# Eight units in flight with tiles laid over one another, and new dates for the last units, in a four-layer graph kernel

One core of one Trainium2 chip. The metric is the device time of one launch in microseconds (us), as the median of several runs. All runs quoted here are of the fast state.

## The reference, cut

Sixty-four graphs of 256 nodes with 128 features go through four layers. Each adds its result to its input and normalises over the features. All is float32.

```
x: (64, 256, 128), adj: (256, 256) zeros and ones
layer 0: h = x Wo; attention scores from a pairing of h.a1 and h.a2, masked, softmax over rows; att h + x Ws
layer 1: h = x W; softmax(leaky_relu(h.a_src + h.a_dst) masked by adj or itself) h; elu
layer 2: five steps of a gated unit:  m = adj h;  z, r = sigmoid(...m..., ...h...);
         hv = tanh(...m..., U5 (r h));  h = (1 - z) h + z hv
layer 3: x W0 + sum over k of adj^k x Wk, k = 1..3
after each layer: x = layernorm(x + layer(x))
```

## The kernel before

A **unit** is two graphs. A **lane** is a set of tiles that holds one unit through all four layers; seven lanes mean seven units in flight. The program is straight-line code. Before it is emitted, a greedy planner in Python puts all instructions in order. For each engine it keeps planned times. When an engine is free, it takes the ready task with the smallest date, `first(t)`. When the last task of a unit is done, its lane gets the next unit. PSUM is the memory that TensorE writes its results to; its eight banks are handed out by the planner in the same way.

```
LANES = 7
LAST_FAR = {0: -1, 1: -1}   # last unit, last but one: the state is turned by TensorE, not by DMA
PERIOD = 43e3
TAIL = 0.1
...
def first(t):                                   # the date of a task: smallest first
    ...
    return (t.unit - (1 - TAIL) * max(t.unit - (NU - LANES), 0)) * PERIOD + t.due
...
zs = [cell(f"z{k}", [P, T]) for k in range(LANES)]          # a tile of its own for each lane's input
...
def spawn(u, lane):
    for k, layer in enumerate((layer0, layer1, layer2, layer3)):
        layer(u, lanes[lane])
        if k == (1 if u < LANES else 0) and u + LANES < NU:
            load_x(u + LANES, after=...)        # next input of this lane: asked for early
...
def lane_cells(k):                              # cut: each name a tile of its own
    c = {name: cell(f"{name}_{k}", [P, T]) for name in ("xT0", "xT1", "ht", "m")}
    c |= {name: cell(f"{name}_{k}", [P, G, N]) for name in ("e", "p")}
    for name, (at, half) in {"r": ("e", 0), "z": ("e", 1), "v": ("p", 0)}.items():
        c[name] = Cell(...)                     # halves of e and p
    c["x"] = cell(...); c["h0"] = cell(f"h0_{k}", [P, G, C0])
```

`t.due` is a task's planned distance from the start of its unit, stretched by up to 1.9. A unit's date is thus its number times 43 us, and the last units' dates are pressed together.

The softmax here doesn't subtract the row's maximum and nothing guards it: scores larger than these inputs give would overflow.

Of the kernel before, what the change touches and what calls it, by code (L numbers as in the profile page):

```python
# [8 lines left out]
F32 = mybir.dt.float32  # L9
AF = mybir.ActivationFunctionType  # L10
ALU = mybir.AluOpType
# [3 lines left out]
NEG = -1.0e30  # L15
EPS = 1e-5
STEPS = 5
LANES = 7
LEAD = 10
BANKS = 8  # L20
BL = 32
FIRST_FAR = {0: 2, 1: 2}
LAST_FAR = {0: -1, 1: -1}
PERIOD = 43e3
TAIL = 0.1
PACE = 1.9
PACE_GATED = 1.56
HOLD = 80
# [6 lines left out]
class Cell:  # L35


    def __init__(self, ap=None, bank=False):
        self.ap, self.bank = ap, bank
        self.writers, self.readers, self.users = [], [], 0  # L40
        self.group, self.waits = None, set()

# [10 lines left out]
class Plan:  # L53
# [17 lines left out]
    def add(self, eng, ns, fn, reads=(), writes=(), after=(), wait=0, group=None, dma=False):  # L71
        t = Task(eng, ns, fn, self.unit, wait, dma or eng == "sp")
        for c in reads:
            t.deps.update(c.writers)
            c.readers.append(t)
        for c in writes:
            if c.bank and not c.writers:
                t.takes.append(c)
            if group is None or c.group is not group:
                c.waits = {*c.writers, *c.readers} - {t}  # L80
                c.writers, c.readers, c.group = [], [], group
            t.deps.update(c.waits)
            c.writers.append(t)
        t.deps.update(after)
        t.deps.discard(t)
        for c in {id(c): c for c in (*reads, *writes) if c.bank}.values():
            c.users += 1
            t.banks.append(c)
        t.step = self.step = self.step + 1
        t.layer = self.layer  # L90
        t.rank = self.rank
        self.tasks.append(t)
        return t
# [4 lines left out]
    def run(self, spawn, units, key):  # L98
# [20 lines left out]
            seen = len(self.tasks)  # L119

        def start(lane):
            if queue:
                self.unit, self.step = queue.pop(0), 0
                lane_of[self.unit] = lane
                spawn(self.unit, lane)

                for t in self.tasks[seen:]:
                    t.due = max([d.due + (PACE_GATED if t.layer == 2 else PACE) * (d.ns + (
                        d.wait + self.LATENCY["sp" if d.dma else d.eng] if d.dma or d.eng != t.eng else self.OWN[t.eng]))
                        for d in t.deps if d.unit == t.unit], default=0.0)  # L130
                enlist()
# [50 lines left out]
def kernel(  # L182
# [55 lines left out]
        return n * (cols * 1.667 + 5)  # L238


    def load(name, src, shape, ns=450, by="sp"):
        c = cell(name, shape)
        queue = {"sp": nc.sync, ACT: nc.scalar}[by]
        add(by, ns, lambda: queue.dma_start(c.ap, src), (), (c,), dma=True)
        return c
# [3 lines left out]
    out_u = out.rearrange("(u b) (c p) d -> u p b c d", b=UB, p=P)  # L249


    zs = [cell(f"z{k}", [P, T]) for k in range(LANES)]

    def load_x(u, by="sp", after=()):
        z = zs[u % LANES]
        if u < LANES:
            queue = {"sp": nc.sync, ACT: nc.scalar}[by]
            add(by, 600, lambda: queue.dma_start(z.ap.rearrange("p (b c d) -> p b c d", b=UB, c=NC), x_u[u]), (), (z,), dma=True, wait=800)
            return
        parts = object()  # L260
        for a in range(D // BL):
            add("sp", 540, lambda a=a: nc.sync.dma_start(
                z.ap[a * BL : (a + 1) * BL].rearrange("j (b i) -> j b i", i=BL),
                x_a[u, a].rearrange("(b j) i -> j b i", j=BL)), (), (z,), after, group=parts)

    w1 = load("w1", W, [D, D])
    load_x(0, ACT)
# [162 lines left out]
    plan.rank = None  # L430


    def lane_cells(k):
        c = {name: cell(f"{name}_{k}", [P, T]) for name in ("xT0", "xT1", "ht", "m")}

        c |= {name: cell(f"{name}_{k}", [P, G, N]) for name in ("e", "p")}
        for name, (at, half) in {"r": ("e", 0), "z": ("e", 1), "v": ("p", 0)}.items():
            c[name] = Cell(c[at].ap.rearrange("p g n -> p (g n)")[:, half * T : (half + 1) * T])
        c["x"] = cell(f"x_{k}", [P, UB, NC, D])
        c["h0"] = cell(f"h0_{k}", [P, G, C0])  # L440
        c |= {name: cell(f"{name}_{k}", [P, G]) for name in ("nm", "s", "rs", "rstd", "ve")}
        c |= {name: cell(f"{name}_{k}", [P, UB]) for name in ("d", "nd")}
        c["st"] = cell(f"st_{k}", [P, UB, 6])
        c["u"] = cell(f"u_{k}", [P, 15])
        c["cu"] = cell(f"cu_{k}", [P, 3, G])
        c["esd"] = cell(f"esd_{k}", [P, 2, G])
        c["hb"] = Cell(dram.tile([P, T], F32, tag=f"hb_{k}", name=f"hb_{k}"))

        for name, n in (("row", T), ("rowu", 2 * T + 2)):
            c[name] = Cell(dram.tile([1, n], F32, tag=f"{name}_{k}", name=f"{name}_{k}"))  # L450
        return c


    X = {}
    lanes = [lane_cells(k) for k in range(LANES)]

    def gd(ap):
        return ap.rearrange("p (g d) -> p g d", g=G)
# [88 lines left out]


    def layer0(u, L):
        xT, z = L["xT0"], zs[u % LANES]  # L550
        if u < LANES:
            feature_major(z, lambda g: gd(z.ap)[:, g], xT)
        else:
# [93 lines left out]
    def layer1(u, L):  # L647
# [17 lines left out]
                    ps_x.ap[:, b * N : (b + 1) * N], X[u].ap[:, b, jc, :], p.ap[:, b * NC + jc, :],  # L665
                    start=(b == 0 and jc == 0), stop=(jc == NC - 1), skip_group_check=True), (X[u], p), (ps_x,))
        add(ACT, 500, lambda: nc.scalar.copy(px.ap, ps_x.ap), (ps_x,), (px,))
        rs, hp, hn, th = L["rs"], L["ht"], L["m"], L["xT1"]
        ex = L["h0"]
        exf = ex.ap.rearrange("p g d -> p (g d)")[:, 0:T]  # L670
        for b in range(UB):
            ps_o = bank()

# [3 lines left out]
            for ic in range(NC):  # L677
# [1 line left out]
                    ov()[:, ic, :], bn(px.ap)[:, b, ic * P : (ic + 1) * P], wx1.ap,  # L679
                    start=(ic == 0), stop=True, skip_group_check=True), (px, wx1), (ps_o,))  # L680
            r = rs.ap[:, b * NC : (b + 1) * NC].rearrange("p (c o) -> p c o", o=1)
            add(DVE, 120, lambda r=r, ov=ov: nc.vector.reciprocal(r, ov()[:, :, D : D + 1]), (ps_o,), (rs,), group=exf)
            add(DVE, 350, lambda b=b, r=r, ov=ov: nc.vector.tensor_mul(
                gd(hp.ap)[:, b * NC : (b + 1) * NC, :], ov()[:, :, 0:D], r.to_broadcast([P, NC, D])), (ps_o, rs), (hp,), group=exf)
        if not u:
            plan.rank = NU
            warm(6, [plan.tasks[-1]])
# [1 line left out]

        add(DVE, 330, lambda: nc.vector.tensor_scalar_min(hn.ap, hp.ap, 0.0), (hp,), (hn,))  # L690
        add(ACT, 550, lambda: nc.scalar.activation(th.ap, hn.ap, AF.Tanh, scale=0.5), (hn,), (th,))
        add(ACT, 550, lambda: nc.scalar.activation(exf, hn.ap, AF.Exp), (hn,), (ex,))
        xf = X[u].ap.rearrange("p b c d -> p (b c d)")
        add(DVE, 600, lambda: nc.vector.scalar_tensor_tensor(hp.ap, hp.ap, 0.0, xf, op0=ALU.max, op1=ALU.add),
            (hp, X[u]), (hp,))
        add(DVE, 600, lambda: nc.vector.scalar_tensor_tensor(th.ap, exf, 1.0, th.ap, op0=ALU.add, op1=ALU.mult),
            (ex, th), (th,))
        add(DVE, 600, lambda: nc.vector.tensor_add(hp.ap, hp.ap, th.ap), (hp, th), (hp,))
        layernorm(u, L, y_pairs(hp))
# [130 lines left out]
    def spawn(u, lane):  # L830
        for k, layer in enumerate((layer0, layer1, layer2, layer3)):
            plan.layer = k
            layer(u, lanes[lane])

            if k == (1 if u < LANES else 0) and u + LANES < NU:
                load_x(u + LANES, after=[plan.tasks[-1]] if k else ())



    def first(t):  # L840
        if t.rank is not None:
            return t.rank * PERIOD
        if t.unit < 0:
            return t.due - 1e6
        return (t.unit - (1 - TAIL) * max(t.unit - (NU - LANES), 0)) * PERIOD + t.due

    with tc.manual_schedule():
        for t in plan.run(spawn, range(NU), first):
# [31 lines left out]
```

## Time and profile before

| | before |
|---|---|
| time | 1434.65 us (1432.92 to 1435.07, 3 runs) |
| span of the profiled run | 1433.4 us |
| TensorE busy | 1419.3 us, 99% |
| VectorE, ScalarE, DMA | 78%, 50%, some 45% |
| records of matmuls and transposes | 5665 |

The engine shares, the windows and the chain around the largest wait are shown in the prediction. To follow where the time goes I use one more reading of the trace: for each matmul, the time from its start to the next matmul's start, less the usual one for its shape (429 ns for 512 columns, 216 for 256, 109 to 113 for 128 to 133; the lower quartile of each shape). What is left over I call **excess**: it holds waits as well as matmuls slowed by a lower clock. The usual times sum to 1409.7 us before.

One line is needed later. It is the view of one source line: the VectorE transpose with which layer 0 of a unit begins (all units but the first seven). The last two numbers before the shape are the first and last start.

```profile
L554 DVE STREAM_TRANSPOSE xT<-z x25: 671/702/706, 183.2 to 1266.2; 128x512 f32<-128x512 f32 x25
```

The last unit begins at 1266.2 us, 167.2 us before the end.

### The profile page before, as it was taken

To read this page: it belongs to the slowest core of one execution; us is meant where nothing else is said; L and a number is where in the kernel's file an instruction comes from. 1 tells how busy PE (TensorE), PEld (TensorE's weight loads), DVE (VectorE), ACT (ScalarE), POOL (GpSimd) and SP (SyncE) were. 2 spreads that over 40 slices of the span, in tenths; PEclk is the share of its full clock that TensorE was granted. 3 is DMA by queue.
4 is the path that set the end of the run, shared out by engine and by line. 5 is a ranking of instruction groups with operands and counts; after the bars stand their busy time and mean duration, and the time that the engine had idled before them with its cause. 6 is when DMAs were issued, how large, how long until landed. Compare 5 with 4: busy or idle time off the path is not lost.

```text
span 1433.4 us, 18429 instructions
## 1 busy us (share of the span) xinstructions
PE 1419.3 (99%) x5665; PEld 960.5 (67%) x5665; DVE 1118.8 (78%) x2597; ACT 718.4 (50%) x1372; POOL 142.1 (10%) x134
## 2 busy tenths in 40 slices
PE   9999999999999999999999999999999999999998
PEld 9666766766666666666666666666666666666676
DVE  7987968788778888778888778887788787677735
ACT  5656445445554545554545545445545454455431
POOL 0110100110001110011110011100011010010102
PEclk9999999999999999999999999999999999999999
DMA  3225564544555454554445454444444444423212
GB/s 93 46 46 109 110 141 102 116 97 107 108 113 123 92 120 102 112 117 111 109 100 115 107 122 111 101 103 104 107 108 105 98 103 93 97 70 81 52 37 59
DMA packets 515170, 141.57 MB, mean 99 GB/s; under 512 B 445056, under 2 KB 481664, under 8 KB 515072
## 3 DMA queue, kind: packets, MB, share of 16 engines
q1 hardware_dynamic: 514272, 139.87, 43.8%
q8 instruction: 46, 0.75, 0.2%
q14 instruction: 52, 0.43, 0.1%
q10 hardware_dynamic: 800, 0.52, 0.1%
HBM read 78.21 MB, written 62.10 MB: 98 GB/s over the span
## 4 chain that ended last, share of the span: by engine, by line
PE 97%; DVE 1%; ACT 1%; issue 0%; POOL 0%; POOLq 0%; DVEq 0%; ACTq 0%
PE ps L726 48%; PE ps L706 23%; PE ps L812 8%; PE ps L634 4%; PE ps L664 4%; PE ps L819 4%; PE ps L678 2%; PE ps L567 2%; PE ps L629 2%; PE ps L781 0%; PE ps L472 0%; ACT e L653 0%; DVE st L526 0%; PE ps L299 0%; PE ps L515 0%
## 5 line engine op out<-in xcount | busy, mean ns | idle before, releaser
L726 PE MATMUL ps<-m,gT 128*128 128x512 f32 x960 | 464.6, 595 | 1.4 <-ACT m L722 1.4
L531 POOL TENSOR_TENSOR rstd<-ve,nhalf 128x4 f32<-128x4 f32 x128 | 141.4, 1108 | 1286.6 <-DVE ve L528 1198.3
L726 PEld LDWEIGHTS ps<-m,gT 128*128 128x128 f32 x960 | 176.3, 190 | 137.1 <-issue 110.5
L706 PE MATMUL ps<-adjTp,ht 128*128 128x256 f32 x928 | 231.0, 380 | 0.0
L706 PEld LDWEIGHTS ps<-adjTp,ht 128*128 128x128 f32 x928 | 176.3, 191 | 65.2 <-issue 42.8
L722 ACT COPY m<-ps 128x512 f32<-128x512 f32 x160 | 93.0, 583 | 182.0 <-PE ps L706 179.0
L741 ACT ACTIVATE e<-ps,bias 128x512 f32<-128x512 f32 x160 | 109.9, 687 | 147.1 <-PE ps L726 147.0
L732 ACT ACTIVATE e<-ps,bias 128x512 f32<-128x512 f32 x160 | 109.7, 687 | 142.2 <-PE ps L726 142.2
L745 DVE TENSOR_TENSOR p<-p,xT 128x512 f32<-128x512 f32 x160 | 109.4, 686 | 85.6 <-ACT p L739 85.4
L734 DVE SCALAR_TENSOR_TENSOR e<-e,xT 128x512 f32<-128x512 f32 x160 | 109.1, 683 | 80.0 <-ACT e L732 72.1
L726 PE MATMUL ps<-xT,gT 128*128 128x512 f32 x320 | 162.8, 593 | 2.7 <-DVE esd L639 2.7
L726 PE MATMUL ps<-e,u5T 128*128 128x512 f32 x320 | 162.8, 592 | 0.0
L739 ACT ACTIVATE p<-ps,bias 128x512 f32<-128x512 f32 x160 | 110.0, 687 | 66.4 <-PE ps L726 59.3
L706 PE MATMUL ps<-adjT,x 128*128 128x256 f32 x512 | 128.8, 379 | 0.0
L706 PEld LDWEIGHTS ps<-adjT,x 128*128 128x128 f32 x512 | 96.2, 190 | 44.9 <-issue 34.2
L746 DVE SCALAR_TENSOR_TENSOR p<-e,p 128x512 f32<-128x512 f32 x160 | 109.2, 683 | 2.0
L748 DVE SCALAR_TENSOR_TENSOR xT<-p,xT 128x512 f32<-128x512 f32 x160 | 109.2, 684 | 1.9
L726 PEld LDWEIGHTS ps<-e,u5T 128*128 128x128 f32 x320 | 60.1, 190 | 38.5 <-issue 28.0
L756 DVE STREAM_TRANSPOSE p<-xT 128x512 f32<-128x512 f32 x116 | 81.2, 701 | 1.2
L726 PEld LDWEIGHTS ps<-xT,gT 128*128 128x128 f32 x320 | 57.1, 190 | 36.6 <-issue 23.7
L653 ACT ACTIVATE e<-m,esd 128x256 f32<-128x256 f32 x112 | 80.4, 763 | 0.4 <-DMA m<-row 0.4
L526 DVE BATCH_NORM_STATS2 st<-ps 128x6 f32<-128x256 f32 x128 | 51.5, 424 | 37.0 <-PE ps L819 22.2
(139 smaller groups left out, 1852.2 us busy)
## 6 DMA issues: line engine op xcount, KB each, us to landing
hb<-p SPq DMA_DIRECT2D x174, 256.0 KB, 2.3
ht<-hb SPq DMA_DIRECT2D x464, 64.0 KB, 2.5
xT<-hb SPq DMA_DIRECT2D x232, 64.0 KB, 2.6
m<-row SPq DMA_DIRECT2D x56, 256.0 KB, 3.9
hb<-p SPq DMA_DIRECT2D x120, 64.0 KB, 1.8
ht<-hb SPq DMA_DIRECT2D x30, 256.0 KB, 2.8
out_dram<-x SPq DMA_DIRECT2D x29, 256.0 KB, 2.7
z<-in_x_dram SPq DMA_DIRECT2D x100, 64.0 KB, 2.4
```

What stands on the lines that cost most here:

```text
L531: add(POOL, 1050, lambda: nc.gpsimd.tensor_tensor(rstd.ap, ve.ap, nhalf.ap, op=ALU.pow), (ve, nhalf), (rstd,))
L706: add(PE, mm_ns(N), lambda b=b, mc=mc: nc.tensor.matmul(ps.ap[:, b * N : (b + 1) * N], lhs(b, mc), mat.ap[:, mc, :], start=(mc == 0), stop ...
L722: add(ACT, 500, lambda ps_m=ps_m: nc.scalar.copy(m.ap, ps_m.ap), (ps_m,), (m,))
L726: add(PE, mm_ns(T), lambda: nc.tensor.matmul(ps.ap, w(), rhs.ap, start=start, stop=stop, skip_group_check=True), (c, rhs), (ps,))
L732: add(ACT, 600, lambda ps_g=ps_g: nc.scalar.activation(r.ap, ps_g.ap, AF.Tanh, bias=bias2.ap[:, 1:2], scale=0.5), (ps_g, bias2), (r,))
L734: add(DVE, 600, lambda h=h: nc.vector.scalar_tensor_tensor(r.ap, r.ap, 1.0, h.ap, op0=ALU.add, op1=ALU.mult), (r, h), (r,))
L739: add(ACT, 600, lambda ps_v=ps_v: nc.scalar.activation(v.ap, ps_v.ap, AF.Tanh, bias=bias2.ap[:, 2:3]), (ps_v, bias2), (v,))
L741: add(ACT, 600, lambda ps_g=ps_g: nc.scalar.activation(z.ap, ps_g.ap, AF.Tanh, bias=bias2.ap[:, 0:1], scale=0.5), (ps_g, bias2), (z,))
L745: add(DVE, 600, lambda h=h: nc.vector.tensor_sub(v.ap, v.ap, h.ap), (v, h), (v,))
L746: add(DVE, 600, lambda: nc.vector.scalar_tensor_tensor(v.ap, z.ap, 1.0, v.ap, op0=ALU.add, op1=ALU.mult), (v, z), (v,))
L748: add(DVE, 600, lambda h=h, new=new: nc.vector.scalar_tensor_tensor(new.ap, v.ap, 0.5, h.ap, op0=ALU.mult, op1=ALU.add), (v, h), (new,))
L812: add(PE, mm_ns(N), lambda k=k, src=src, c=c, b=b: nc.tensor.matmul(view(c)[:, :, b, :], bn(src.ap)[:, b, c * P : (c + 1) * P], w3.ap[:, k ...
```

## The change

Its intent: more units in flight, so that TensorE always finds something ready. Eight lanes with a tile for each name do not fit: the build of the old kernel with eight lanes stops with

```
Not enough space for pool "const" with 214.0625 kb per partition ... There was 207.8740234375 kb per partition left
```

This agrees with the Trainium skill, "SBUF — State Buffer", Specifications (TRN2), which gives about 208 KiB as usable. So tiles with disjoint lifetimes are laid over one another. `Cell` learns of overlaps (`over`), and a writer waits for the users of all cells that overlap.

```diff
-LANES = 7
+LANES = 8
-LAST_FAR = {0: -1, 1: -1}
+LAST_FAR = {0: -1, 1: 1}
-TAIL = 0.1
+TAIL = 0.3
+LATE = 5
@@ Cell, Plan.add
-                c.waits = {*c.writers, *c.readers} - {t}
+                c.waits = {w for o in (c, *c.over) for w in (*o.writers, *o.readers)} - {t}
@@ Plan.run, start: a lane now takes only the units u with u % LANES == lane
-            if queue:
-                self.unit, self.step = queue.pop(0), 0
+            mine = [u for u in queue if u % LANES == lane]
+            if mine:
+                self.unit, self.step = mine[0], 0
+                queue.remove(self.unit)
@@ lanes: h0 shares with ht; r, ex and z, th are halves of e; v and xT1 are halves of p
-        c = {name: cell(f"{name}_{k}", [P, T]) for name in ("xT0", "xT1", "ht", "m")}
+        c = {name: cell(f"{name}_{k}", [P, T]) for name in ("xT0", "m")}
+        wide = sb(f"ht_{k}", [P, G * C0])
+        c["ht"] = Cell(wide[:, 0:T])
+        c["h0"] = Cell(wide.rearrange("p (g d) -> p g d", g=G), over=[c["ht"]])
+        for at, halves in (("e", (("r", "ex"), ("z", "th"))), ("p", (("v",), ("xT1",)))): ...
@@ the input lies in m and is asked for at the unit's end
-    zs = [cell(f"z{k}", [P, T]) for k in range(LANES)]
-        z = zs[u % LANES]
+        z = lanes[u % LANES]["m"]
-            if k == (1 if u < LANES else 0) and u + LANES < NU:
-                load_x(u + LANES, after=[plan.tasks[-1]] if k else ())
+        if u + LANES < NU:
+            load_x(u + LANES)
@@ dates
-        return (t.unit - (1 - TAIL) * max(t.unit - (NU - LANES), 0)) * PERIOD + t.due
+        return (t.unit if t.unit < NU - LANES else NU - 1 - LATE - (NU - 1 - t.unit) * TAIL) * PERIOD + t.due
```

The dates of units 24 to 31, in periods, are 24.0, 25.0, 25.1 ... 25.6 by the old formula with seven lanes, 24.0, 24.1 ... 24.7 by the old formula with eight, and 23.9, 24.2, 24.5 ... 26.0 by the new one.

The tie of units to lanes is needed because the input now lies in a tile of the lane. It is one more difference between the two kernels, but no rival. The planner runs without the chip: run again for the kernels of the old rule that are quoted here, it gives unit `u` to lane `u % LANES` anyway, and in the kernels of the new rule the lane that is waited for is also the first to be free.

More of the change, by code (lines that the diff above doesn't have):

```diff
@@ L35, with __init__ @@
 class Cell:
-    def __init__(self, ap=None, bank=False):
+    def __init__(self, ap=None, bank=False, over=()):
         self.ap, self.bank = ap, bank
+        self.over = list(over)
+        for c in over:
+            c.over.append(self)
         self.writers, self.readers, self.users = [], [], 0
@@ L238, in mm_ns, with lane_cells @@
         return n * (cols * 1.667 + 5)
+    def lane_cells(k):
+        c = {name: cell(f"{name}_{k}", [P, T]) for name in ("xT0", "m")}
+        wide = sb(f"ht_{k}", [P, G * C0])
+        c["ht"] = Cell(wide[:, 0:T])
+        c["h0"] = Cell(wide.rearrange("p (g d) -> p g d", g=G), over=[c["ht"]])
+        c |= {name: cell(f"{name}_{k}", [P, G, N]) for name in ("e", "p")}
+        for at, halves in (("e", (("r", "ex"), ("z", "th"))), ("p", (("v",), ("xT1",)))):
+            for half, names in enumerate(halves):
+                over = [c[at]]
+                for name in names:
+                    c[name] = Cell(c[at].ap.rearrange("p g n -> p (g n)")[:, half * T : (half + 1) * T], over=over)
+                    over = [*over, c[name]]
+        c["x"] = cell(f"x_{k}", [P, UB, NC, D])
+        c |= {name: cell(f"{name}_{k}", [P, G]) for name in ("nm", "s", "rs", "rstd", "ve")}
+        c |= {name: cell(f"{name}_{k}", [P, UB]) for name in ("d", "nd")}
+        c["st"] = cell(f"st_{k}", [P, UB, 6])
+        c["u"] = cell(f"u_{k}", [P, 15])
+        c["cu"] = cell(f"cu_{k}", [P, 3, G])
+        c["esd"] = cell(f"esd_{k}", [P, 2, G])
+        c["hb"] = Cell(dram.tile([P, T], F32, tag=f"hb_{k}", name=f"hb_{k}"))
+        for name, n in (("row", T), ("rowu", 2 * T + 2)):
+            c[name] = Cell(dram.tile([1, n], F32, tag=f"{name}_{k}", name=f"{name}_{k}"))
+        return c
+    lanes = [lane_cells(k) for k in range(LANES)]
     def load(name, src, shape, ns=450, by="sp"):
@@ L249, with load_x @@
     out_u = out.rearrange("(u b) (c p) d -> u p b c d", b=UB, p=P)
-    zs = [cell(f"z{k}", [P, T]) for k in range(LANES)]
-    def load_x(u, by="sp", after=()):
-        z = zs[u % LANES]
+    def load_x(u, by="sp"):
+        z = lanes[u % LANES]["m"]
         if u < LANES:
@@ L263, in load_x @@
                 z.ap[a * BL : (a + 1) * BL].rearrange("j (b i) -> j b i", i=BL),
-                x_a[u, a].rearrange("(b j) i -> j b i", j=BL)), (), (z,), after, group=parts)
+                x_a[u, a].rearrange("(b j) i -> j b i", j=BL)), (), (z,), group=parts)
     w1 = load("w1", W, [D, D])
@@ L430 @@
     plan.rank = None
-    def lane_cells(k):
-        c = {name: cell(f"{name}_{k}", [P, T]) for name in ("xT0", "xT1", "ht", "m")}
-        c |= {name: cell(f"{name}_{k}", [P, G, N]) for name in ("e", "p")}
-        for name, (at, half) in {"r": ("e", 0), "z": ("e", 1), "v": ("p", 0)}.items():
-            c[name] = Cell(c[at].ap.rearrange("p g n -> p (g n)")[:, half * T : (half + 1) * T])
-        c["x"] = cell(f"x_{k}", [P, UB, NC, D])
-        c["h0"] = cell(f"h0_{k}", [P, G, C0])
-        c |= {name: cell(f"{name}_{k}", [P, G]) for name in ("nm", "s", "rs", "rstd", "ve")}
-        c |= {name: cell(f"{name}_{k}", [P, UB]) for name in ("d", "nd")}
-        c["st"] = cell(f"st_{k}", [P, UB, 6])
-        c["u"] = cell(f"u_{k}", [P, 15])
-        c["cu"] = cell(f"cu_{k}", [P, 3, G])
-        c["esd"] = cell(f"esd_{k}", [P, 2, G])
-        c["hb"] = Cell(dram.tile([P, T], F32, tag=f"hb_{k}", name=f"hb_{k}"))
-        for name, n in (("row", T), ("rowu", 2 * T + 2)):
-            c[name] = Cell(dram.tile([1, n], F32, tag=f"{name}_{k}", name=f"{name}_{k}"))
-        return c
     X = {}
-    lanes = [lane_cells(k) for k in range(LANES)]
     def gd(ap):
@@ L549, in layer0 @@
     def layer0(u, L):
-        xT, z = L["xT0"], zs[u % LANES]
+        xT, z = L["xT0"], L["m"]
         if u < LANES:
@@ L667, in layer1 @@
         add(ACT, 500, lambda: nc.scalar.copy(px.ap, ps_x.ap), (ps_x,), (px,))
-        rs, hp, hn, th = L["rs"], L["ht"], L["m"], L["xT1"]
-        ex = L["h0"]
-        exf = ex.ap.rearrange("p g d -> p (g d)")[:, 0:T]
+        rs, hp, hn, th = L["rs"], L["ht"], L["m"], L["th"]
+        ex, parts = L["ex"], object()
         for b in range(UB):
@@ L681, in layer1 @@
             r = rs.ap[:, b * NC : (b + 1) * NC].rearrange("p (c o) -> p c o", o=1)
-            add(DVE, 120, lambda r=r, ov=ov: nc.vector.reciprocal(r, ov()[:, :, D : D + 1]), (ps_o,), (rs,), group=exf)
+            add(DVE, 120, lambda r=r, ov=ov: nc.vector.reciprocal(r, ov()[:, :, D : D + 1]), (ps_o,), (rs,), group=parts)
             add(DVE, 350, lambda b=b, r=r, ov=ov: nc.vector.tensor_mul(
-                gd(hp.ap)[:, b * NC : (b + 1) * NC, :], ov()[:, :, 0:D], r.to_broadcast([P, NC, D])), (ps_o, rs), (hp,), group=exf)
+                gd(hp.ap)[:, b * NC : (b + 1) * NC, :], ov()[:, :, 0:D], r.to_broadcast([P, NC, D])), (ps_o, rs), (hp,), group=parts)
         if not u:
@@ L691, in layer1 @@
         add(ACT, 550, lambda: nc.scalar.activation(th.ap, hn.ap, AF.Tanh, scale=0.5), (hn,), (th,))
-        add(ACT, 550, lambda: nc.scalar.activation(exf, hn.ap, AF.Exp), (hn,), (ex,))
+        add(ACT, 550, lambda: nc.scalar.activation(ex.ap, hn.ap, AF.Exp), (hn,), (ex,))
         xf = X[u].ap.rearrange("p b c d -> p (b c d)")
@@ L695, in layer1 @@
             (hp, X[u]), (hp,))
-        add(DVE, 600, lambda: nc.vector.scalar_tensor_tensor(th.ap, exf, 1.0, th.ap, op0=ALU.add, op1=ALU.mult),
+        add(DVE, 600, lambda: nc.vector.scalar_tensor_tensor(th.ap, ex.ap, 1.0, th.ap, op0=ALU.add, op1=ALU.mult),
             (ex, th), (th,))
```

## The prediction

> **What bounds the kernel now.** I read the page first: the engines' shares, the 40 slices and the chain that ended last. Then the groups of TensorE by shape, the windows of 50 us, the waits of TensorE, the chain in order of time around the largest wait, and the timeline of the last 20 us.
>
> ```profile
> PE 1419.3 (99%) x5665; PEld 960.5 (67%) x5665; DVE 1118.8 (78%) x2597; ACT 718.4 (50%) x1372; POOL 142.1 (10%) x134
> PE   9999999999999999999999999999999999999998
> PE 97%; DVE 1%; ACT 1%; issue 0%; POOL 0%; POOLq 0%; DVEq 0%; ACTq 0%
> ```
>
> TensorE is busy for 99% of the span in all slices, and the chain runs through it for 97%. A busy TensorE is not yet one at its peak, so I ask whether the matmuls come as closely as they can. The chain in order of time has runs of equal matmuls, whose length over their number is the time from one start to the next:
>
> ```profile
> 15.83 1.75 PE ps L472 x16
> ...
> 29.33 1.82 PE ps L567 x16
> ...
> 115.52 1.79 PE ps L634 x16
> 117.31 1.73 PE ps L706 x8
> 119.03 3.43 PE ps L726 x8
> ```
>
> From the last line up: 0.429 us for 512 columns, 0.216 for 256, 0.112 for 130, 0.114 for 133, 0.109 for a transpose. The groups by shape give the counts. 1600 matmuls of 512 columns (960 + 320 + 320) make 686 us. 2560 of 256 columns (L706 1536, L664 256, L812 512, L819 256) make 553. 1024 of 129 or 130 make 115, and 256 of 133 make 29. Some 140 transposes make 15. The 20 warming matmuls and the small ones make about 11. Sum: about **1409 us** of the span of 1433.4. Per unit (1/32 of the first four terms) it is 43.2 us, and in the middle of the run the same piece of the chain (L706 x10) comes at 659.74, 703.02, 746.32: a period of 43.29. So in the steady state nothing but TensorE sets the time, and it is at its full pace. What can still be won is 24 us at most, and it lies in a few places. The windows show them (columns: busy of PE, PEld, DVE, ACT, POOL; clock; DMA share; GB/s):
>
> ```profile
> 0.00:50.00 50.00, 47.41 (x324) 43.05 (x325) 39.36 (x142) 28.41 (x79) 5.96 (x11) 1.00 0.31 76
> 150.00:200.00 50.00, 49.49 (x184) 33.49 (x183) 42.02 (x97) 19.62 (x34) 8.17 (x7) 1.00 0.59 126
> 600.00:650.00 50.00, 49.02 (x198) 32.89 (x198) 41.14 (x96) 25.64 (x54) 4.30 (x4) 1.00 0.46 103
> 1100.00:1150.00 50.00, 49.15 (x188) 32.23 (x187) 40.35 (x88) 26.60 (x49) 3.02 (x3) 1.00 0.45 101
> 1150.00:1200.00 50.00, 47.28 (x179) 31.12 (x179) 36.68 (x87) 20.85 (x40) 5.92 (x5) 0.97 0.44 101
> 1400.00:1450.00 50.00, 26.98 (x128) 23.02 (x126) 19.87 (x58) 5.08 (x13) 7.11 (x7) 0.95 0.16 42
> ```
>
> TensorE idles 2.6 us at the start, 0.5 at 150 to 200, 1.0 at 600 to 650, 0.85 and 2.7 between 1100 and 1200, and 6.4 at the end (33.4 - 26.98). All other windows have 50.00. The largest wait in the run is this (chain in order of time, left out between):
>
> ```profile
> 1187.48 0.98 DVE st L526 x3
> ...
> 1188.66 1.02 POOL rstd L531
> ...
> 1190.75 0.16 DVE esd L639
> ...
> 1190.95 2.90 PE ps L726 x4
> 1193.85 2.51 PE ps L706 x8
> ```
>
> A matmul of layer 2 waits for L639, a VectorE instruction of another unit's layer 0 which it doesn't read: it waits for that unit's PSUM bank. Two layer norms met at 1188. After 2.7 us of idleness the next twelve matmuls take 5.41 us in place of 3.45 (4 x 0.429 + 8 x 0.216), and the window's clock is 0.97. The wait costs **2.7 + 2.0 us**. The end is a dependent tail: the last matmuls start at 1425.02, then come statistics, the power on GpSimd, the scaling, and the store at 1430.10.
>
> **What the Trainium skill says.** "TensorE: Matmul & The Clock Gate", section "Wait — 56ns, not 53.3ns?", gives the warm start-to-start time as N / 2.4 GHz plus about 2.5 ns. The trace agrees if fp32 passes twice: 1024 / 2.4 + 2.5 = 429 ns, which is what is measured, so there is no pace left to win. The same page's Part 1 says that an idle window of some 3.4 us halves the clock until TensorE has been busy again; the slow matmuls after 1190.95 agree, and so do the first eight of the run (L299 x8 in 3.78 us, not 1.73). "PSUM — Partial Sum Buffer", Specifications: 8 banks. The kernel uses all eight before and after, so one more unit in flight gets no more of them. "DMA: Bandwidth & Descriptors", section "Latency and other measured facts", puts a fixed cost of about 2 us on a transfer; the input loads land 1.9 to 4.4 us after issue (median 2.4), which agrees.
>
> **The change, part by part.**
> 1. Seven lanes become eight. A lane's unit may now take 8 x 43.3 = 346 us in place of 303. In the steady state TensorE is full with seven, so this is worth nothing there. What it can do is give the order more units to choose from near the places where TensorE waited.
> 2. Laying over. The input goes into `m`, `h0` shares with `ht`, `xT1` is the second half of `p`, and the two results of layer 1 lie in `e`. Within a unit these are used one after another anyway: `e` has been multiplied into `p` before `ex` and `th` are written, and `p` has been read by L664 before layer 2 writes `v` or `xT1`. I count no new wait inside a unit. Between units there is one: the load of the lane's next unit used to be issued during a unit's early layers, hundreds of us early, and now it must follow the last read of `m` in layer 3 (L812). After that read come L819, the layer norm and the store, some 7 us by the timeline of the end; the four pieces of the load need about 2 us to issue and 2.4 to land. So they are there at about the time when the lane is given on, and seven other units cover the rest: **0 us**.
> 3. Transposes. Unit 7 is now a first-round unit with its input transposed on TensorE: 4 more. Unit 30 gets its state back by DMA at two points (before step 0 and after step 0) where it used TensorE: 8 fewer. Net -4 x 0.109 = **-0.4 us**; x5665 becomes x5661.
> 4. Dates. The last seven units stood 0.1 period (4.3 us of planned time) apart, and the last eight now stand 0.3 (13 us) apart. Planned time runs up to 1.9 times the true latency, so neighbours end some 7 us apart, not 2. That spreads the layer norms of the tail, which met at 1188, but leaves less to interleave in the last 20 us, where TensorE is now full up to 1425. I count the good side in the sum below, and **up to +3 us** for the other.
> 5. The starting 5 us (cold clock, loads) and the last 6.4 us have the same instructions as before: 0.
>
> The sum: reachable are the waits at 150, 600, 1100 and 1190, 0.5 + 1.0 + 0.85 + 2.7 = 5.1 us, and the 2.0 of clock, 7.1 in all. A new order throws these dice again. They are rare events of a static order that meets true durations: ACT's L653 lasts 763 ns where the kernel plans 600, and the waits at 630 and 1102 follow bunches of it. So I take 60% of the 7.1 as won, 4.3, plus 0.4 of transposes: 4.7 us. 1434.65 - 4.65 = **1430.0 us**.
>
> **The rivals.**
> *The tail is better filled and every wait goes.* For it: all idle time outside the ends is in five spots, two in the tail whose dates are new. Against: PSUM has no more banks, and ACT's bunches stay. It would give 1434.65 - 7.1 - 0.4 = 1427.2; some of the start's 2.6 us as well, about 1425.
> *The spacing starves TensorE at the end.* With 13 us between units the last two or three run almost alone. A layer 2 step alone is a chain of about 9 us with 3 us of matmuls in it (5 x 0.429 + 4 x 0.216). For it: before, the last windows are full just because all units end together. Against: layer 3 is dense (28 x 0.216 = 6.0 us) and unit 31 keeps its transposes on TensorE. It would cost 3 to 8 us and leave 1434 to 1438.
> *New waits for banks or for the late load.* If a lane's next unit starts late, or the load's wait holds up the in-order queue of SP behind it, single waits of 1 to 3 us would appear each period. For it: that queue carries nearly all transfers. Against: DMA is 45% busy and the planner orders by what is ready. If it took 0.5 us in each of 24 periods it would be +12 us, 1442; I give it one in twenty.
>
> **Range and chances.** TensorE's 1409 us and the two ends (1.4 + 6.4 us, and about 5 us of start) put the floor at about 1422, so faster by over 2% (under 1406) is impossible without fewer matmuls: 0.005. Slower by over 2% (over 1463) would take a wait of 1 us in each period: 0.01. The range 1425 to 1436 reaches from nearly all waits gone to the starving tail without its worst.
>
> **What would show it.** Right: x5661 on TensorE; a period of 43.3 us in the middle; no wait over 1.5 us between 1000 and 1400; no window at clock 0.97 but the last; 6 to 7 us from the last matmul to the end. Part 4 wrong: the last two windows lose some us of TensorE. Part 2 wrong: waits behind L554 or the load, period after period, and a period over 43.4. The whole would be wrong if the steady period fell well under 43.2, since that would mean that TensorE's pace was not the bound.

## The result

| | before | after |
|---|---|---|
| time, median | 1434.53 us (1432.92 to 1435.07, 6 runs) | 1428.60 us (1427.97 to 1429.24, 6 runs) |
| span of the profiled run | 1433.4 | 1426.8 |

The ratio is 0.9961, 95% interval 0.9948 to 0.9974. Ratios here are the mean time of one kernel's fast runs over that of the other's of the same rounds, so not quite the ratio of the medians. The prediction of 1430.0 was 1.4 us too high and its range held. In another set of runs the kernel after gave 0.9960.

The share line of the page after has the four transposes fewer:

```profile
PE 1416.4 (99%) x5661; PEld 960.0 (67%) x5661; DVE 1122.3 (79%) x2598; ACT 719.1 (50%) x1371; POOL 135.9 (10%) x134
```

The windows of the kernel after (busy of PE, PEld, DVE, ACT, POOL; clock; DMA share; GB/s), those that answer to the ones in the prediction and two new ones:

```profile
100.00:150.00 50.00, 49.40 (x193) 31.52 (x192) 38.07 (x83) 31.51 (x55) 3.02 (x3) 1.00 0.43 96
...
300.00:350.00 50.00, 49.32 (x195) 32.23 (x193) 44.22 (x103) 28.29 (x58) 3.02 (x3) 1.00 0.50 110
...
600.00:650.00 50.00, 50.00 (x206) 34.26 (x205) 41.99 (x95) 24.91 (x48) 4.06 (x4) 1.00 0.50 105
...
1150.00:1200.00 50.00, 50.00 (x186) 31.88 (x185) 37.29 (x83) 26.14 (x48) 3.02 (x3) 1.00 0.46 100
...
1400.00:1450.00 50.00, 20.25 (x97) 17.05 (x95) 12.38 (x38) 4.00 (x9) 5.04 (x5) 0.94 0.07 21
```

The wait at 631 and the window of 47.28 are gone. Two windows early in the run now have 0.6 and 0.7 us of idle that were not there. The waits of TensorE after (total, times, longest):

```profile
PE ps L336 <- POOL ident masks.py:199: 1.4, 1, 1.4
PE ps L740 <- ACT m L736: 0.7, 1, 0.7
PE ps L720 <- DVE esd L654: 0.6, 1, 0.6
```

The 1.4 is the first instruction of the kernel. No other single wait is above 0.7 us; before, the largest was 2.7. The period in the middle, from the chain in order of time:

```profile
661.22 3.43 PE ps L740 x8
...
704.43 3.43 PE ps L740 x8
...
747.63 3.43 PE ps L740 x8
```

It is 43.20 to 43.21 us, where it was 43.29. And the last unit begins five microseconds earlier:

```profile
L569 DVE STREAM_TRANSPOSE xT<-m x24: 677/702/734, 186.1 to 1261.2; 128x512 f32<-128x512 f32 x24
```

The whole span, taken apart by excess:

| us | before | after | won |
|---|---|---|---|
| all matmuls at the usual pace | 1409.7 | 1409.2 | 0.4 |
| first matmul begins at | 1.4 | 1.4 | 0 |
| excess 0 to 100 | 5.4 | 4.6 | 0.8 |
| excess 100 to 400 | 1.3 | 2.8 | -1.4 |
| excess 400 to 1000 | 2.7 | 0.3 | 2.5 |
| excess 1000 to 1200 | 6.0 | 1.5 | 4.5 |
| excess 1200 to the last matmul | 0.5 | 0.5 | 0 |
| last matmul to the end | 6.4 | 6.5 | -0.1 |
| span | 1433.4 | 1426.8 | 6.7 |

(The first 100 us vary by run: the same kernel after has 4.0 in its second profile, so the 0.8 is partly chance. The other rows repeat within 0.1.)

So the gain is where the prediction looked for it: the tail, the middle, the transposes. Its signs of being right came true as well: x5661, no wait over 1.5 us between 1000 and 1400, a clock of 1.00 in every window but the last, 6.5 us after the last matmul. All that says where, not which part of the change. For that the parts were taken one by one.

### The profile page after: what moved, and what is told of

It is laid out like the page before. It is cut to its first block, busy times and chain, and to the rows that moved or that the text cites. A ratio compares the mean times of both kernels' runs of the same rounds, so it can differ in the third digit from the quotient of the medians.

```text
span 1426.8 us, 18452 instructions
## 1 busy us (share of the span) xinstructions
PE 1416.4 (99%) x5661; PEld 960.0 (67%) x5661; DVE 1122.3 (79%) x2598; ACT 719.1 (50%) x1371; POOL 135.9 (10%) x134
## 4 chain that ended last, share of the span: by engine, by line
PE 98%; DVE 1%; ACT 0%; issue 0%; POOL 0%; POOLq 0%; DVEq 0%
PE ps L740 48%; PE ps L720 23%; PE ps L826 8%; PE ps L649 4%; PE ps L833 4%; PE ps L679 4%; PE ps L644 2%; PE ps L692 2%; PE ps L582 2%; PE ps L795 0%; PE ps L487 0%; DVE st L541 0%; PE ps L336 0%; PE ps L530 0%; PE ps L607 0%
## 5 line engine op out<-in xcount | busy, mean ns | idle before, releaser
L546 POOL TENSOR_TENSOR rstd<-ve,nhalf 128x4 f32<-128x4 f32 x128 | 135.2, 1058 | 1286.1 <-DVE ve L543 1117.8
L720 PE MATMUL ps<-adjT,x 128*128 128x256 f32 x512 | 134.9, 379 | 0.0
L748 DVE SCALAR_TENSOR_TENSOR e<-e,xT 128x512 f32<-128x512 f32 x96 | 65.6, 684 | 45.2 <-ACT e L746 44.5
L759 DVE TENSOR_TENSOR p<-p,xT 128x512 f32<-128x512 f32 x96 | 65.0, 677 | 44.5 <-ACT p L753 44.5
L740 PE MATMUL ps<-xT,gT 128*128 128x512 f32 x192 | 98.0, 593 | 0.0
L668 ACT ACTIVATE e<-m,esd 128x256 f32<-128x256 f32 x112 | 77.5, 758 | 0.0
L649 PEld LDWEIGHTS ps<-ht,p 128*128 128x128 f32 x512 | 67.4, 190 | 6.9 <-issue 3.8
L679 PEld LDWEIGHTS ps<-p,x 128*128 128x128 f32 x256 | 48.2, 190 | 32.7 <-issue 28.2
L649 PE MATMUL ps<-ht,p 128*128 128x130 f32 x512 | 69.8, 274 | 0.1
```

Of the source, the lines that this page charges most:

```text
L546: add(POOL, 1050, lambda: nc.gpsimd.tensor_tensor(rstd.ap, ve.ap, nhalf.ap, op=ALU.pow), (ve, nhalf), (rstd,))
L649: add(PE, mm_ns(D + 2), lambda b=b, ic=ic, kc=kc, yv=yv: nc.tensor.matmul(yv()[:, ic, :], p.ap[:, b * NC + kc, ic * P : (ic + 1) * P], h.a ...
L668: add(ACT, 600, lambda g=g, b=b: nc.scalar.activation(e.ap[:, g, :].rearrange("p (c n) -> p c n", c=NC), ev()[:, b], AF.Prelu, bias=esd.ap ...
L679: add(PE, mm_ns(N), lambda b=b, jc=jc: nc.tensor.matmul(ps_x.ap[:, b * N : (b + 1) * N], X[u].ap[:, b, jc, :], p.ap[:, b * NC + jc, :], st ...
L720: add(PE, mm_ns(N), lambda b=b, mc=mc: nc.tensor.matmul(ps.ap[:, b * N : (b + 1) * N], lhs(b, mc), mat.ap[:, mc, :], start=(mc == 0), stop ...
L740: add(PE, mm_ns(T), lambda: nc.tensor.matmul(ps.ap, w(), rhs.ap, start=start, stop=stop, skip_group_check=True), (c, rhs), (ps,))
```

## The experiments

Each was timed against the kernel before in five rounds (four to six runs), those of one set on the same chip. "Retuned" dates are the best pair of TAIL and LATE, of some thirty for each variant, by the planner's own clock; that clock chose what to run and is used for no time here. "Last start" is the last start of layer 0's input transpose, "rest" is the span less that. Excess is in us, over the stretches named.

| run | lanes | tiles | dates | time | ratio, 95% | last start | rest | excess 100-400 / 400-1000 / 1000-1200 / 1200-end |
|---|---|---|---|---|---|---|---|---|
| before | 7 | own | old | 1434.5 | 1 | 1266.2 | 167.2 | 1.3 / 2.7 / 6.0 / 0.5 |
| after | 8 | laid over | new | 1428.6 | 0.9961 (0.9948, 0.9974) | 1261.2 | 165.6 | 2.8 / 0.3 / 1.5 / 0.5 |
| e1_dates | 7 | own | new | 1443.1 | 1.0062 (1.0050, 1.0074) | 1263.4 | 177.9 | 1.3 / 2.8 / 3.2 / 12.2 |
| e2_lanes | 8 | laid over | old | 1446.1 | 1.0074 (1.0058, 1.0090) | 1289.6 | 155.6 | 2.8 / 0.6 / 0.1 / 19.5 |
| e3_overlay | 7 | laid over | old | 1457.8 | 1.0162 (1.0148, 1.0175) | 1299.4 | 156.5 | 2.7 / 3.5 / 3.2 / 24.4 |
| e4_lastfar | 8 | laid over | new | 1429.9 | 0.9968 (0.9956, 0.9980) | 1260.4 | 167.3 | 2.8 / 0.3 / 1.5 / 0.5 |
| e13_start | 8 | laid over | old, unit 23 earlier | 1431.9 | 0.9977 (0.9965, 0.9990) | 1242.3 | 188.2 | 2.8 / 1.7 / 2.0 / 1.5 |
| e14_seven | 7 | own | retuned | 1429.9 | 0.9962 (0.9950, 0.9975) | 1256.6 | 171.0 | 1.3 / 2.7 / 1.0 / 1.5 |
| e6_early | 8 | only xT1 laid over | new | 1427.2 | 0.9942 (0.9930, 0.9955) | 1267.2 | 157.3 | 1.0 / 0.3 / 1.1 / 1.4 |
| e15_best | 8 | laid over | retuned | 1427.0 | 0.9946 (0.9933, 0.9960) | 1251.1 | 174.2 | 2.8 / 0.3 / 1.1 / 0.5 |
| e17_overlay_dates | 7 | laid over | retuned | 1434.0 | 0.9995 (0.9981, 1.0008) | 1262.0 | 170.1 | 2.7 / 3.5 / 3.7 / 1.1 |
| e9_nine | 9 | laid over | retuned | 1431.2 | 0.9976 (0.9964, 0.9989) | 1252.0 | 177.5 | 5.0 / 0.5 / 1.2 / 0.5 |
| after_again | 8 | laid over | new | 1428.8 | 0.9960 (0.9947, 0.9972) | 1260.5 | 165.6 | 2.8 / 0.3 / 1.5 / 0.5 |
| e16_combo | 8 | only xT1 laid over | retuned | 1425.8 | 0.9940 (0.9927, 0.9952) | 1253.5 | 169.7 | 1.0 / 0.3 / 0.2 / 0.8 |

My theory at the start: the tail's gain is the dates', the middle's is the eighth lane's, and laying over is free. The rivals: it takes eight lanes for all of it; or any new order shakes the waits anew and the gain is luck.

### First set: the parts alone

**e1_dates**: the kernel before with the new dates only.

```diff
-TAIL = 0.1
+TAIL = 0.3
+LATE = 5
-        return (t.unit - (1 - TAIL) * max(t.unit - (NU - LANES), 0)) * PERIOD + t.due
+        return (t.unit if t.unit < NU - LANES else NU - 1 - LATE - (NU - 1 - t.unit) * TAIL) * PERIOD + t.due
```

> The kernel before, seven lanes, with only the new dates of the last seven units. If the two late waits (0.85 us at 1102, 2.7 + 2.0 us at 1190) went because of the dates, as my step 4 and the trace after suggest (excess over full pace between 1000 and 1200 us: 6.0 before, 1.5 after), it gains 4 to 5 us: about 1430, with the waits at 166 and 631 and the 0.08 us hiccup of each period still there. If eight lanes are what removes them, it stays at 1434.5 within 1 us. If seven lanes with the wider spacing starve TensorE at the end, it is above 1435.

Measured: 1443.1 us, **slower** by 0.6%, the third of the three cases. The 1000 to 1200 stretch improved (6.0 to 3.2), but 12.2 us were lost at the very end. The chain in order of time, at that end:

```profile
1418.66 1.00 DVE p L486
...
1421.90 0.37 SPq L825
...
1422.31 0.54 SPq L492
...
1424.26 2.31 DMA xT<-hb
...
1426.70 6.44 PE ps L813 x16
```

One unit is left, and its state goes the long way: turned by VectorE, out to DRAM, back in by four transfers, then the products of layer 3. TensorE waits 7.3 us, and the sixteen products after it take 6.44 us in place of 3.45 because the clock fell (0.64 granted from 1425 to 1435). Units 30 and 31 are turned by TensorE in this kernel (`LAST_FAR`), so the straggler is an earlier unit, overtaken by them. The planner's order, laid beside the trace, names it: unit 29 ends at 1438.5, units 30 and 31 at 1390.5 and 1421.2. This is the starving rival of the prediction, in a form that I had not thought of.

**e2_lanes**: the kernel after with the old dates and the old `LAST_FAR`, so the eighth lane and the laid-over tiles.

```diff
-LAST_FAR = {0: -1, 1: 1}
+LAST_FAR = {0: -1, 1: -1}
-TAIL = 0.3
-LATE = 5
+TAIL = 0.1
-        return (t.unit if t.unit < NU - LANES else ...) * PERIOD + t.due
+        return (t.unit - (1 - TAIL) * max(t.unit - (NU - LANES), 0)) * PERIOD + t.due
```

> The kernel after with the old dates (last eight units 0.1 period apart) and the old LAST_FAR: eight lanes and the laid-over tiles alone. Lanes-theory: 1429.5, only the 0.9 us of transposes short of the kernel after. Dates-theory: it wins the start (0.8), the wait at 631 and the hiccups (2.4) and loses 1.4 at 100 to 350, but keeps some 4.5 us of waits in the tail: about 1433. Dice: anything between 1429 and 1437, with waits at places where neither kernel has them.

Measured: 1446.1 us, outside all three. From 1000 to 1200 us no other run is as smooth (0.1 us of excess), and that with the old dates: the new dates are not needed to lose the waits at 1102 and 1190. Then it loses 19 at the end. Its end, from the chain in order of time:

```profile
1416.48 5.42 PE ps L739 x8
1421.93 0.70 ACT p L752
1422.65 0.70 DVE p L758
1423.38 0.70 DVE p L759
1424.10 0.70 DVE p L761
...
1424.85 0.67 PE ps L794 x4
```

That is the gate of one layer 2 step, instruction after instruction, with no other unit's matmul between: the last unit is alone, at a lowered clock (0.75 from 1415 to 1425; 5.42 us for eight matmuls that take 3.43). It began late:

```profile
L568 DVE STREAM_TRANSPOSE xT<-m x24: 665/704/723, 186.2 to 1289.6; 128x512 f32<-128x512 f32 x24
```

**e3_overlay**: as e2_lanes, with `LANES = 7`: only the tiles, the load and the tie of units to lanes differ from the kernel before.

```diff
-LANES = 8
+LANES = 7
```

> The kernel after with seven lanes, old dates and old LAST_FAR: only the laid-over tiles and the late input load are left of the change. If the late load is free, as I predicted, the period stays 43.2 to 43.3 and the time 1434.5 within 2 us. If a lane's next unit now starts late and seven lanes do not cover it, there are waits of TensorE each period: 1437 or more. It also shows how much a mere change of order moves the time.

Measured: 1457.8 us, +1.6%. Not by waits in each period: the excess from 400 to 1000 is 3.5 us against 2.7. It loses 24 us after 1350, again with the last unit alone:

```profile
L568 DVE STREAM_TRANSPOSE xT<-m x25: 669/705/712, 184.5 to 1299.4; 128x512 f32<-128x512 f32 x25
```

The late load is not what held it up. These are the loads of the inputs (first and last issue, time to landing), and VectorE just before the last start:

```profile
L298 SPq DMA_DIRECT2D m<-in_x_dram x100: 312/487/1888, 171.6 to 1271.3; - x100
DMA to landing us min/median/max: 1.8/2.3/4.7
```

```profile
1298.14 1.36 DVE L554 TENSOR_SCALAR x<-ps,st,rstd 128x128 f32<-128x128 f32 x4
1299.41 0.70 DVE L568 STREAM_TRANSPOSE xT<-m 128x512 f32<-128x512 f32 x1
```

The last load was there by 1276, 23 us early. The start follows at once on the last layer norm of the unit that had the lane, unit 24 in the planner's order. That unit took 368 us from its first to its last VectorE instruction, where it took 333 in the kernel before.

**e4_lastfar**: the kernel after with the old `LAST_FAR`.

```diff
-LAST_FAR = {0: -1, 1: 1}
+LAST_FAR = {0: -1, 1: -1}
```

> The kernel after with the old LAST_FAR: unit 30 is turned by TensorE again, 8 more transposes of 0.109 us. x5669 on TensorE. If only these count: 1429.5 (+0.9). If the shorter latency of the TensorE path had mattered for the end, it would be equal or below 1428.6; if the order's dice decide, anything within 3 us.

Measured: 1429.9 us, ratio 0.9968 against 0.9961; the span is 1.0 us longer and the excess the same. Eight transposes of 0.109 us make 0.9. This part is what I took it for.

So each large part alone makes the kernel slower, by 8.6 to 23 us, and together they make it 5.9 us faster. No sum of parts explains that. The column "rest" suggested a better theory: **a unit needs about 156 us from its layer 0 to the end, however few others compete**. e2 and e3 ended 155.6 and 156.5 us after their last start, and no run has less. (In other runs another unit can end last. By the planner's order unit 31 itself takes 152.7 to 162.0 us, from its first to its last VectorE instruction, in all fourteen profiles of the table.) So, by estimate, a last unit that begins after about 1269 (1425 - 156) makes the end late by the difference, whatever else TensorE has to do. The planner lets units with close dates share TensorE, so pressing the last dates together would slow the older unit whose lane the last one waits for. The second set tests this.

### Second set: the last start

**e13_start**: e2_lanes with one date moved, that of unit 23, whose lane passes to unit 31.

```diff
-        return (t.unit - (1 - TAIL) * max(t.unit - (NU - LANES), 0)) * PERIOD + t.due
+        return (t.unit - (1 - TAIL) * max(t.unit - (NU - LANES), 0) - 0.5 * (t.unit == NU - LANES - 1)) * PERIOD + t.due
```

> The run of eight lanes with the old dates and the old LAST_FAR (1446 us) with one date moved: unit 23, whose lane passes to unit 31, half a period earlier. In the traces unit 31's first vector instruction is at 1266 (before), 1261 (after), 1290 (that run), 1299 (seven lanes laid over), and the two late ones end 156 us after it. Theory of the last start: unit 31 starts before 1262, the waits of unit 31's chain at the end go, 1429 to 1431. Rival (close dates as such, or its transposes on TensorE, starve the end): no gain, 1440 or more.

Measured: 1431.9 us, 14 us less than e2_lanes, by half a period in one unit's date. The last start moved from 1289.6 to 1242.3, and the excess after 1200 fell from 19.5 to 1.5:

```profile
L568 DVE STREAM_TRANSPOSE xT<-m x24: 669/703/739, 186.1 to 1242.3; 128x512 f32<-128x512 f32 x24
```

It is 0.9 us over the range I gave: the new order has four new waits of 0.7 to 0.8 us between 967 and 1238. The rival is out: close dates do not starve the end by themselves, a late last start does.

**e14_seven**: seven lanes and own tiles, dates retuned, new `LAST_FAR`.

```diff
-TAIL = 0.1
+TAIL = 0.15
+LATE = 4.5
-LAST_FAR = {0: -1, 1: -1}
+LAST_FAR = {0: -1, 1: 1}
-        return (t.unit - (1 - TAIL) * max(t.unit - (NU - LANES), 0)) * PERIOD + t.due
+        return (t.unit if t.unit < NU - LANES else NU - 1 - LATE - (NU - 1 - t.unit) * TAIL) * PERIOD + t.due
```

> The kernel before, seven lanes and its own tiles, with other dates of the new form (TAIL 0.15, LATE 4.5) and the new LAST_FAR. Theory of the dates: the tail's waits go with seven lanes too (4.5 us), the 0.9 us of transposes as well, while the wait at 631 and the hiccups of 0.08 us per period stay: 1429 to 1431. Theory that it takes eight units in flight: 1434 or more.

Measured: 1429.9 us, ratio 0.9962, the same as the kernel after (0.9961 and 0.9960, in other rounds). Its windows:

```profile
600.00:650.00 50.00, 49.03 (x200) 32.94 (x199) 41.13 (x96) 25.45 (x52) 4.31 (x4) 1.00 0.47 104
1100.00:1150.00 50.00, 49.76 (x196) 33.35 (x195) 41.27 (x90) 26.16 (x49) 5.20 (x4) 1.00 0.44 104
1150.00:1200.00 50.00, 50.00 (x189) 32.85 (x189) 39.36 (x88) 25.45 (x47) 4.59 (x4) 1.00 0.46 106
```

The 49.15 and 47.28 of before are 49.76 and 50.00, while 600 to 650 still has its 49.03. **A gain of this size does not need the eighth lane or the laid-over tiles.** The tail's excess is 1.0 + 1.5 with seven lanes. The wait at 631 and the small ones of each period are still there (2.7 in the middle), but between 100 and 400 it has only 1.3, where every run with all tiles laid over, of seven lanes or more, has 2.7 or more.

**e6_early**: eight lanes, but only `xT1` laid over `p`, which is enough to fit. The input keeps its own tile and is asked for early. Dates and `LAST_FAR` as after.

```diff
 # against the kernel before
-LANES = 7
+LANES = 8
-        c = {name: cell(f"{name}_{k}", [P, T]) for name in ("xT0", "xT1", "ht", "m")}
+        c = {name: cell(f"{name}_{k}", [P, T]) for name in ("xT0", "ht", "m")}
-        ... {"r": ("e", 0), "z": ("e", 1), "v": ("p", 0)}
+        ... {"r": ("e", 0), "z": ("e", 1), "v": ("p", 0), "xT1": ("p", 1)}
 # and the dates and LAST_FAR of the kernel after
```

> Eight lanes with only xT1 laid over p, which already makes room; the input keeps its own tile and is loaded a lane's life ahead, as before; dates and LAST_FAR of the kernel after. If the late load into m costs nothing with eight lanes, as predicted: 1428.6 within 1.5 us, with the start, the middle and the period of 43.2 as in the kernel after. If it costs: 1426 or less.

Measured: 1427.2 us, ratio 0.9942. By the time that is the lower edge of my first case; by the ratio it is 0.2% better than the kernel after (whose ratio was taken in other rounds). The excess from 100 to 400 is 1.0 in place of 2.8, so laying everything over, with the late load, comes with 1.8 us there. But two of the three waits that vanished (at 119 and 159 us) lie before the first lane is handed on (186 us), so they can't be waits for the late load; they come with another order. Nor is the load waited for later: in the kernel after, the view of the 24 input transposes (L569) lists no idle time of VectorE before any of them. The rest of 157.3 is at the limit, and still the excess at the end is only 1.4.

**e15_best**: the kernel after with other dates.

```diff
-TAIL = 0.3
-LATE = 5
+TAIL = 0.35
+LATE = 4.5
```

> The kernel after with TAIL 0.35 and LATE 4.5 in place of 0.3 and 5. If the order is chaotic in the dates: anything from 1427 to 1440. If the kernel after stands near the bottom of a flat valley: 1428.6 within 1 us, and the waits between 1000 and 1200 stay near 1.5 us, since PSUM's banks set them.

Measured: 1427.0 us, ratio 0.9946, 1.6 us under the kernel after where I had allowed 1, though the intervals of the two overlap widely. These neighbouring dates do as well as those of the kernel after; that speaks for a flat valley, though one pair is all that was run near it.

### Third set: all lessons together

**after_again**: the kernel after, as the yardstick.

> The kernel after, unchanged, as the yardstick for the others on the same chip: 0.996 of the kernel before, about 1428.6.

Measured: 1428.8 us, 0.9960.

**e17_overlay_dates**: e3_overlay with dates retuned and the new `LAST_FAR`.

```diff
 # against the kernel after
-LANES = 8
+LANES = 7
-TAIL = 0.3
-LATE = 5
+TAIL = 0.25
+LATE = 4
```

> Seven lanes with all tiles laid over (1457.8 with the old dates) with dates TAIL 0.25 and LATE 4 and the new LAST_FAR. Theory of the last start: unit 31 starts before 1270 where it started at 1299, and most of the 23 us goes: 1432 to 1437. Rival (laying over makes seven lanes wait in themselves): above 1445.

Measured: 1434.0 us, 23.8 us less than e3_overlay, with the last start at 1262.0 in place of 1299.4. Nearly all of what laying over seemed to cost with seven lanes was a late last start. What remains against e14_seven, 4 us, is spread over waits before 1200.

**e9_nine**: nine lanes fit, too.

```diff
 # against the kernel after
-LANES = 8
+LANES = 9
-TAIL = 0.3
-LATE = 5
+TAIL = 0.35
+LATE = 5.5
```

> The kernel after with nine lanes, dates TAIL 0.35 and LATE 5.5. TensorE is at full pace between 400 and 1000 with eight, so a ninth lane can win nothing there; it adds four transposes of the first round (0.4 us): 1427 to 1431. If more units in flight as such shorten the run: 1425 or less.

Measured: 1431.2 us, ratio 0.9976, at the upper edge of the first case. The middle is as full as with eight (0.5), and the start is worse (5.0 from 100 to 400). A ninth lane does not shorten the run.

**e16_combo**: e6_early with dates retuned.

```diff
-TAIL = 0.3
-LATE = 5
+TAIL = 0.4
+LATE = 4
```

> Eight lanes, only xT1 laid over, the input in its own tile and loaded early, with dates TAIL 0.4 and LATE 4. If the early load's saving (1.8 us of excess between 100 and 350, seen in the run with the early load) stays and the dates keep the tail under 1.5 us of excess: 1426 to 1427, the fastest so far, with unit 31 starting before 1262. If the date valley is rough: up to 1432.

Measured: 1425.8 us, ratio 0.9940, on the same rounds in which the kernel after had 0.9960. It is the fastest of all, 3.0 us under the kernel after in medians. The two intervals touch (0.9952 and 0.9947), but each is taken against the kernel before, whose own times scatter. Set side by side, all five runs of this kernel (1425.05 to 1427.42) lie below all five of the kernel after (1428.04 to 1429.40), and the profiles agree (spans 1423.3 and 1426.1). Its tail has no idle time left, by the windows:

```profile
1000.00:1100.00 100.00, 100.00 (x402) 68.67 (x401) 86.67 (x205) 50.15 (x95) 11.62 (x11) 1.00 0.47 104
1100.00:1200.00 100.00, 100.00 (x361) 63.50 (x361) 76.59 (x165) 52.17 (x96) 7.98 (x7) 1.00 0.47 103
1200.00:1300.00 100.00, 100.00 (x362) 63.27 (x361) 73.69 (x152) 48.33 (x84) 8.09 (x7) 1.00 0.44 99
1300.00:1400.00 100.00, 100.00 (x395) 69.71 (x394) 62.11 (x138) 39.34 (x68) 11.24 (x11) 1.00 0.19 45
```

What it has left over the usual pace is 6.2 us of excess, 3.9 of it in the first 50 us, and the two ends of 1.4 and 6.5.

## Why the prediction was right, and where it was not

**The bound** was right. TensorE at its usual pace makes 1409 us, no span was under 1423, and the floor of "about 1422" stood. x5661 is what the page shows.

**Part 1** (the eighth lane is worth nothing in the steady state) was wrong, by 2 to 3 us. From 400 to 1000 the kernel after won 2.5 us: the wait of 1.1 us at 631 and a delay of some 0.08 us in each period (43.29 to 43.20). The step that failed is "TensorE is full with seven": at 43.29 it was not quite. It is the lane and not the tiles, for with own tiles (e14_seven and e6_early) that stretch is 2.7 with seven lanes and 0.3 with eight. Those two ran in the same rounds, both with dates of the new form, and took 1429.9 and 1427.2 us with no overlap of their runs. The kernel after hides most of this, because with all tiles laid over it lost 1.4 us between 100 and 400.

**Part 2** (laying over costs 0 us) was right about the load and wrong about the whole. The load lands before its lane is free (in e3_overlay 23 us before, for the last unit), and there is no wait in each period. But between 100 and 400 the excess is 2.7 and 2.8 with all tiles laid over (e3_overlay with seven lanes, the kernel after with eight) and 1.3 and 1.0 without (the kernel before, e6_early). And with seven lanes and the old dates the run took 23 us more, because unit 24 ran 36 us longer and the last start came 33 us later. The step that failed is the one that goes from "no new wait inside a unit" and "seven other units cover the rest" to 0 us: it counts waits of the old order, while the new dependencies make another order, in which the unit that the last one waits for can be slower. At the end no other unit covers that.

**Part 3** (transposes, -0.4 net) was right: 1409.7 to 1409.2, and e4_lastfar shows the 0.9 of unit 30's eight.

**Part 4** (dates: the good side in the sum, up to 3 us for the bad) got the net right for the combination, but neither side as I saw it. The good side: the tail won 4.5 us, and 4.0 with seven lanes and dates of the new form (e14_seven: 6.0 + 0.5 became 1.0 + 1.5). But e2_lanes has 0.1 us between 1000 and 1200 with the old dates, so with eight lanes the late waits go without the new dates too; what these won there is the last start and the 19 us at the end. The bad side was 0 in the kernel after, but 12 us in e1_dates. I reasoned about how much work is left when the last units end one after another. What decides is when the last unit begins, and whether a unit that goes by DMA ends last; neither stood in my estimate.

Two counts in it were wrong, too. The trace shows each fp32 matmul as two records (the 25 products of 512 columns in a unit's layer 2, times 32, are 800, and the records are 1600). So a step has 10 x 0.429 + 8 x 0.216 = 6.0 us of matmuls, not 3, and layer 3 has 32 records of 256 columns, 6.9 us, not 28 and 6.0. The last step of e3_overlay, with no other unit's matmul in it, takes 9.6 us from its first matmul (L719 at 1426.60) to the transposes of its result (L794 at 1436.17), and in the step before it was 2.25 us from there to the next step. So, by estimate, a step alone takes some 12 us, and two units in layer 2 nearly fill TensorE. That would explain why the wide spacing starved nothing in the kernel after; it was not tested by itself. The sums of the prediction are of records and stand.

**The 60%** was a guess that came out a little low: of the 7.1 us of waits and clock, the kernel after removed those at 631 and 1190, halved the one at 1102, and made new ones of 1.4 us net between 100 and 400. That the total came within 1.4 us is in part luck: Part 1 gave 2.5 us that were expected only in part, Part 2 took 1.4 that were not, and the end, which lost 12 to 24 us in e1_dates, e2_lanes and e3_overlay, lost nothing in this one combination. The reason for the 60% was wrong. I called the waits rare events of a static order that meets true durations. They are not events but parts of the order: the wait at 631 is 1.14 us in all three kernels whose order is the same up to there (before, e1_dates, e14_seven: 1.138, 1.142, 1.136), and the one at 323 is 0.84 us in five runs with eight laid-over lanes (after, e2_lanes, e4_lastfar, e13_start, e15_best: 0.838 or 0.839). An order repeats to a hundredth of a microsecond; only a new order throws again.

**The rivals.** The first (all waits go) is close to what e16_combo reaches. The second (starving at the end) did not happen in the kernel after and did in e1_dates, e2_lanes and e3_overlay; the last two had the old, close dates, so there it was not the spacing. The third (waits for banks or the load in each period) happened in no run: none of the runs with the late load shows idle time of VectorE before an input transpose.

What stays open: why the order between 100 and 400 us is worse with all tiles laid over, and why unit 24 takes longer in e3_overlay. A direct wait for the late load is ruled out for both; whether shared tiles hold a unit up themselves, or only make the planner choose another order, was not separated. With other dates unit 24 takes 325 us on the same tiles (e17_overlay_dates).

## What to carry to other kernels

When one engine is full in the middle of a run, look at the ends first; count back from the end how long one work item needs alone, and see that the last item starts before that. In a greedy order by date the item that must finish first is the one whose buffers the last item waits for: giving it half a period in its date was worth 14 us here. Parts of a change that all act on one order do not add up, so test them together and each alone, and tune the plain variant as well before crediting the larger one.

## What the Trainium skill lacked or had wrong

- "TensorE: Matmul & The Clock Gate", Part 1, lets the clock fall after an idle window of about 3.4 us. Here a shorter wait was enough, and the length of the wait did not settle it. In the kernel before the clock fell after a wait of 2.7 us (the next twelve matmuls took 5.41 us, not 3.45). After a wait of 1.9 us in e1_dates (at 1199) and one of 3.0 in e3_overlay (at 1408) the next matmuls kept the usual pace. The prediction called the slow matmuls after 1190.95 an agreement with the page; in the halved pace they are, in the length of the wait they are not.
- No page says that a trace shows an fp32 matmul as two records, which halves a count of work by instructions of the program. The runs show 1600 records of 429 ns for 800 products of 512 columns, 0.86 us each. That agrees with the four passes that "FP8 and Floating Point Precision", TensorE Precision Notes, gives for true fp32 (by estimate 4 x 512 / 2.4 = 853 ns, with the 2.4 GHz of the formula in the prediction); the two passes of my prediction are those of one record.
